# A two-layer transformer on one core: a norm moved across a layer's end, roots and evictions reordered, and one weight load split in ten

## The chip, the core and the metric

The kernel runs on one NeuronCore of a Trainium2 chip. The metric is the device time of one execution in microseconds (us), lower is better. The core has four engines that compute and that run side by side: TensorE (PE in the profile; PEld are its weight loads), VectorE (DVE), ScalarE (ACT) and GpSimd (POOL). A fifth, SyncE (SP), issues loads and stores here. Each engine takes its instructions in the order of its own queue and waits where an operand isn't ready. TensorE writes its products to PSUM, a small memory of banks, from where ScalarE or VectorE copy them out ("evict" them); a bank can be used again only when that is done.

## The reference

`x` is 4 x 512 x 256. Everything is in 32-bit floats. Each of two layers adds an attention and a feed-forward part, both behind a normalisation without weights:

```python
x = x + _L0_attn_ref(_layernorm(x, axis=-1), w_project, w_out)
x = x + _L0_ffn_ref(_layernorm(x, axis=-1), router_w, router_b, expert_w, expert_b)
x = x + _L1_attn_ref(_layernorm(x, axis=-1), w_qkv, w_proj)
x = x + _L1_ffn_ref(_layernorm(x, axis=-1), gate_W_packed, gate_scales, ...)
```

Layer 0's attention is causal, with 16 heads of 16, over 512 positions. Layer 0's feed-forward has 8 experts and a router that gives, for each row and each of the 256 output columns, 8 logits; the two greatest are kept with their softmax weights:

```python
logits = (h @ router_w.T + router_b).reshape(T, O, E)
w, sel = top_k(softmax(logits), 2)
w = w / sum(w)                       # c: these weights, at their experts
final = einsum('te,teo->to', c, einsum('th,eoh->teo', h, expert_w) + expert_b)
```

Layer 1's attention has 16 query heads of 128 in 4 groups, each group with one key and value head. It attends over the first axis of its input, which here has 4 places, so each softmax is over 4 scores. Layer 1's feed-forward multiplies with weights given as packed 4-bit codes and block scales, with a GELU and a gate between.

## The kernel before

**Tiling.** The 2048 rows are 16 groups of 128 (`g`), and 4 blocks of 4 groups (`j` or `b`). `xres` holds the running sum of all of them in the core's memory from beginning to end. A norm is made for one block: `norm_pieces` (line 187) has four statistics pairs on VectorE (L197, L198), a reciprocal root, and four subtract-and-multiply `xn` (L211). The root starts with three small VectorE operations (`rsqrt_guess`) and goes on with ten more (`rsqrt_steps`, L174 to L183) on the engine it is given: GpSimd unless `eng` says VectorE. Then TensorE transposes `xn` in two halves (L227), and ScalarE copies them to `xT` (L294 and L292 in layer 0, L905 in layer 1).

**Order.** TensorE, VectorE and GpSimd run in the order in which the program emits instructions; from layer 1 on ScalarE does too (in layer 0 the framework orders ScalarE). That order comes from a planner. Work that may be put between other work is written as generators, each held in a `Stream`: before a piece it yields `need(engine, cost, gap, cond)`. A call of `fill` (line 140) begins a new slot, gives TensorE and VectorE a budget of microseconds, emits what was deferred, and goes through `streams` in order: a stream may go on while its engine has budget left, at least `gap` slots have passed since its last piece, and `cond` holds. A budget may be overdrawn by one piece, and the debt is carried over. `defer` puts off a ScalarE instruction to the beginning of the next fill. `normed` is a lock: only one norm lies between its statistics and its transposes at a time.

**Layer 0.** 44 batches of attention run through a fixed sequence (scores `s`, their row maxima `mx` at L653, the shift of the queries at L669, scores again, exponentials L692, mixing `av`), with two fills in each. `divided` (line 731) finishes one sequence's heads: transposes, reciprocal and product on VectorE, transposes, and, after the last sequence of a block, two output products (L764) that are added to `xres` (L773). Then `hidden_pieces(j)` normalises that block for the experts. Streams run beside this: `logit_pieces` (products `lg_ps`, evicted to `lg`), `weight_pieces` (line 371, VectorE: the two greatest of 8 logits and their weights, 17 counted pieces a group), `result_pieces` (expert products `eo`, evicted into `part` with the weights as factors, L339), and `addition_pieces` (L366 to L368). Expert and router products go two experts at a time, 512 columns wide, four matmuls each. They continue until far into layer 1 and are the filler between its own steps.

In `weight_pieces` the gap between the two greatest logits (L401) goes through a tanh and a scaling on ScalarE (`lesser`, L405 and L406, put off by one fill); VectorE reads `th` at L421 and `w1` at L434.

After the last batch, a loop of fills runs until the last `divided` is through. Layer 0's memory is then released, and `w_qkv` (two loads of 1536 KB, one for each half of its rows) and `w_proj` (one of 2048 KB) are loaded into its place.

**Layer 1.** `start_pieces(j)` (line 908) normalises block `j`, transposes it and makes the values `v` (L919). It must be through before the block's first of 4 steps `p = 4 j + kv`; block 0's stands at the very beginning, with fills around it, and `hidden_pieces(3)`, inserted just before, shares the norm's lock with it. A step projects four query heads and a key (`project1`, L937, evicted by ScalarE to `qT` and `kT`), scores, softmax, `mix` (line 999: products `a` in four PSUM tiles, one for each quarter of the rows, then four ScalarE copies to `oT`), and `output` (L1025). In the loop over `p` (line 1073) the output of `p` and the projections of `p + 1` alternate, with a fill (`between`) after each. `qk_ps`, `v_ps`, `lg_ps`, `eo` and the transposes share two PSUM buffers (`ps_dn`): each of them waits until the one before the last has been evicted.

When layer 0's experts are through, `weight_in_pieces` begins to unpack the packed weights for layer 1's feed-forward (`dequant_pieces`, line 833): of a piece, two ScalarE operations, `over` (L855) and `sign` (L860), are put off by one fill each.

Of the kernel before, what the change touches and what calls it, by code (L numbers as in the profile page):

```python
# [32 lines left out]
def tile_transformer(  # L33
# [77 lines left out]
    def need(engine, cost, gap=0, cond=None):  # L111
        return engine, cost, gap, cond
# [18 lines left out]
    streams = []  # L131
    deferred = []

    def defer(emit):

        deferred.append((slot, emit))

    left = {"PE": 0.0, "DVE": 0.0}

    def fill(**budget):  # L140

        nonlocal slot
        slot += 1
        while deferred and deferred[0][0] < slot:
            deferred.pop(0)[1]()
        for engine, b in budget.items():
            left[engine] = min(left[engine], 0.0) + b
        again = True
        while again:
            again = False  # L150
            for stream in list(streams):
                while stream.ready(left):
                    engine, cost = stream.go()
                    left[engine] -= cost
                    again = True
                if stream.next is None:
                    streams.remove(stream)
# [26 lines left out]

    normed = []

    def norm_pieces(j, pool, small, out, deinterleave=False, eng=None, cond=None):

        yield need("DVE", 1.0, cond=lambda: not normed and (cond is None or cond()))
        normed.append(j)  # L190
        st = small.tile([P, 4, 6], F32, tag="ln_st", name=f"ln_st{j}")
        mv = small.tile([P, 4, 2], F32, tag="ln_mv", name=f"ln_mv{j}")
        rs = small.tile([P, 4], F32, tag="ln_rs", name=f"ln_rs{j}")
        for t in range(4):
            if t == 2:
                yield need("DVE", 1.0)
            nc.vector.bn_stats(st[:, t, :], xres[:, 4 * j + t, :])  # L197
            nc.vector.bn_aggr(mv[:, t, :], st[:, t, :])  # L198
        eng = eng or nc.gpsimd
        yield need("DVE", 0.6 if eng is nc.gpsimd else 2.6)  # L200
        v = rsqrt_guess(rs, mv[:, :, 1], small, j)
        rsqrt_steps(eng, rs, v, small, j)
        xn = pool.tile([P, 4, HID], F32, tag="xn", name=f"xn{j}")
        for t in range(4):
            if t % 2 == 0:
                yield need("DVE", 0.9, 2 if not t and eng is nc.gpsimd else 0)
            src, dst = xres[:, 4 * j + t, :], xn[:, t, :]
            if deinterleave:
                src = src.rearrange("p (k two) -> p two k", two=2)
                dst = dst.rearrange("p (two k) -> p two k", two=2)  # L210
            nc.vector.tensor_scalar(  # L211
                dst, src, mv[:, t, 0:1], rs[:, t : t + 1], ALU.subtract, ALU.mult
            )
        out.append(xn)
# [66 lines left out]
    def hidden_pieces(b):  # L281

        out = []
        done = (4 * b - 5, 1)
        yield from norm_pieces(b, b1, b2, out, cond=lambda: b < 2 or done in halves)
        xT = b2.tile([P, 2, 512], F32, tag="xT", name=f"xT{b}")
        for hc in range(2):
            yield need("PE", 0.5, 1 - hc)
            ps = transposed(out[0], hc, ps_dn, "dn", f"xT_ps{b}_{hc}")
            ps = ps.rearrange("p t q -> p (t q)")  # L290
            if hc:
                nc.scalar.activation(xT[:, hc, :], ps, AF.Identity, bias=last_16)  # L292
            else:
                nc.scalar.copy(xT[:, hc, :], ps)  # L294
        normed.clear()
        xTs[b] = xT
# [74 lines left out]
    def weight_pieces():  # L371

        tt, stt = nc.vector.tensor_tensor, nc.vector.scalar_tensor_tensor
        for g in range(NT):
            yield need("DVE", 1.25, cond=lambda: g in logits and logits[g][1] < slot)
            d = logits[g][0]
# [27 lines left out]
            def lesser(th=th, gap=gap, w1=w1):  # L404
                nc.scalar.activation(th, gap, AF.Tanh, scale=0.5)  # L405
                nc.scalar.activation(w1, th, AF.Identity, bias=half_t, scale=0.5)  # L406

            defer(lesser)
            for e in (0, 4):
                yield need("DVE", 1.25)  # L410
                tt(  # L411
# [3 lines left out]

            yield need("DVE", 0.7, 1)
            owing = b5.tile([P, HID], F32, tag="owing", name=f"owing_{g}_")
            nc.vector.tensor_scalar(gap, gap, 0.0, -1.0, ALU.is_equal, ALU.mult)  # L420
            stt(owing, th, -1.0, gap, ALU.add, ALU.add)  # L421
# [19 lines left out]
            stt(c1, sums[:, :NE], 0.5, c1, ALU.mult, ALU.add)  # L441
            weights[g] = c1, slot
            del logits[g]

# [6 lines left out]
    with ExitStack() as l0:  # L451
# [343 lines left out]
        for n in range(NBT):  # L795
# [29 lines left out]
            if n in (2, 6):  # L825
                load_x(n // 4 + 2)
        mixed(NBT - 1)
        last = Stream(divided(*batches[NBT - 1][:2]))
        streams.insert(0, last)
        while last.next is not None:  # L830
# [2 lines left out]
    def dequant_pieces(pool, once, n, packed, scales, to, defer=defer):  # L833

        wi = pool.tile([P, 2, HID], I32, tag="dq_w", name=f"dq_w{n}")
        sc = pool.tile([P, 2, HID], F32, tag="dq_s", name=f"dq_s{n}")
        for i in range(2):  # L840
            nc.sync.dma_start(out=wi[:, i], in_=packed[i])
            for b in range(8):
                nc.sync.dma_start(out=sc[16 * b : 16 * b + 16, i], in_=scales[i](b))
        mi = once.tile([P, 2, 2, HID], I32, tag="dq_m", name=f"dq_m{n}")
        si = once.tile([P, 2, 2, HID], I32, tag="dq_i", name=f"dq_i{n}")
        a = once.tile([P, 2, 2, HID], F32, tag="dq_a", name=f"dq_a{n}")
        over = once.tile([P, 2, 2, HID], F32, tag="dq_b", name=f"dq_b{n}")
# [12 lines left out]
        defer(lambda: nc.scalar.activation(sign, si, AF.Identity, bias=half_t, scale=-0.125))  # L860
        yield need("DVE", 1.25)
        stt(a, mi, 4.0, mi, ALU.max, ALU.add)
        yield need("DVE", 1.25, 1)
        stt(a, a, -4.0, over, ALU.add, ALU.add)
        yield need("DVE", 1.25)
        tt(a, a, sign, ALU.mult)
        yield need("DVE", 1.3)
        tt(to, a, sc.unsqueeze(2).to_broadcast([P, 2, 2, HID]), ALU.mult)
# [16 lines left out]
    with ExitStack() as l1:  # L885
        in_order.enter_context(tc.manual_schedule(engines={mybir.EngineType.Activation}))
        wb = l1.enter_context(tc.tile_pool(name="w_l1", bufs=1))
        wqkv = wb.tile([P, 2, NKV, HPK + 2, P], F32, name="wqkv")
        for hc in range(2):
            nc.sync.dma_start(out=wqkv[:, hc], in_=w_qkv[hc * P : (hc + 1) * P])  # L890
        wpj = wb.tile([P, NKV * HPK, HID], F32, name="wpj")
        nc.sync.dma_start(out=wpj, in_=w_proj.rearrange("(e p) h -> p e h", p=P))
        c1 = l1.enter_context(tc.tile_pool(name="l1_1", bufs=1))
# [6 lines left out]
        def into_T(out, to, name):  # L900

            for hc in range(2):
                yield need("PE", 0.5, 1 - hc)
                ps = transposed(out[0], hc, ps_dn, "dn", f"{name}_ps{hc}")
                nc.scalar.copy(to[:, hc, :], ps.rearrange("p t q -> p (t q)"))  # L905
            normed.clear()

        def start_pieces(j):

            out = []  # L910
            yield from norm_pieces(j, c1, c1, out, cond=lambda: (4 * j + 3, 1) in added)
            xT = c2.tile([P, 2, 512], F32, tag="xT", name=f"xT1_{j}")
            yield from into_T(out, xT, f"xT1_{j}")
            v = c2.tile([P, 4, NKV, P], F32, tag="v", name=f"v{j}")
# [84 lines left out]
        def mix(p):  # L999
# [10 lines left out]
                    )  # L1010
            oT = c2.tile([P, HPK, 512], F32, tag="oT", name=f"oT{p}")
            oq = oT.rearrange("p h (t c q) -> p c t h q", c=NC, q=32)
            for c in range(NC):
                nc.scalar.copy(oq[:, c], avs[c])
            state["o"] = oT

        def output(p, t):

# [54 lines left out]
        for p in range(-1, NP):  # L1073
# [22 lines left out]
            for h in range(HPK + 1):  # L1096
                if h == 2 and p >= 0:
                    mix(p)
                    if not new:
                        first_products()  # L1100
                if new:
                    project1(p + 1, h)
                    between()
            for t in range(4):
                if p >= 0:
# [20 lines left out]
    with ExitStack() as f1:  # L1126
# [9 lines left out]
        def inner(j):  # L1136
            xT = normed_T(j, d2, d2, ps_dn, "dn", deinterleave=True) if j else x_first
            it = d2.tile([P, NJ, 2, 512], F32, tag="it", name=f"it{j}")
            for jj in range(NJ):
# [21 lines left out]
                if j < 2 and jj % 4 == 3:  # L1161
                    at = 4 * j + 2 * (jj // 4)
                    for _ in dequant_pieces(
                        d2, d1, f"d{at}", [down_w[at + i] for i in range(2)],
                        [
                            lambda b, i=i: down_s[at + i, b : b + 1, :].to_broadcast([16, HID])
                            for i in range(2)
                        ],
                        wd[:, at : at + 2], lambda emit: emit(),
                    ):  # L1170
                        pass
            return it
# [85 lines left out]
```

## Time and profile before

| | us |
|---|---|
| median of 3 runs | 1230.52 (1230.14 to 1233.79) |
| the profiled execution | 1231.27 |
| its span | 1229.6 |

Busy time by stretch, of the profiled execution:

| stretch, us | what runs | PE | DVE | ACT | PE clock |
|---|---|---|---|---|---|
| 0 to 165 | attention of layer 0, first blocks | 141.7 | 90.0 | 55.2 | 0.95 |
| 165 to 403 | attention with router and experts | 228.2 | 204.5 | 130.4 | 0.99 |
| 403 to 431 | end of layer 0 | 23.2 | 21.5 | 13.6 | 1.00 |
| 431 to 491 | start of layer 1 | 50.9 | 35.7 | 21.9 | 0.86 |
| 491 to 745 | attention of layer 1 with experts | 251.7 | 169.8 | 113.1 | 0.99 |
| 745 to 900 | attention of layer 1 with unpacking | 150.9 | 102.5 | 62.4 | 1.00 |
| 900 to 1229.6 | feed-forward of layer 1 | 325.6 | 188.6 | 87.1 | 1.00 |

How to read the profile: one execution was recorded instruction by instruction. Times count from the start of the span. L12 is line 12 of the kernel. "out<-in" names what an instruction writes and reads. The "releaser" of an idle time is the instruction whose end let the waiting one go. The clock is the share of TensorE's full clock that it was granted. DVE is VectorE, ACT is ScalarE, POOL is GpSimd, SP is SyncE.

### The profile page before, as it was taken

What the parts mean: (1) busy time and instruction counts of PE and PEld (TensorE: products, weight loads), DVE (VectorE), ACT (ScalarE), POOL (GpSimd) and SP (SyncE); (2) the same over time, 40 slices, a digit from 0 to 9 for tenths busy, and PEclk for the clock granted to TensorE, in tenths of its full rate; (3) what the DMA queues carried; (4) which work ended last, traced back from release to release, by engine and by line L of the source; (5) the groups of instructions that cost most, each with busy time, mean ns of one, the idle gap of its engine ahead of it and who ended that gap; (6) DMA issues with size and microseconds to landing.
All of it is one profiled execution on the core that took longest, in us unless ns stands there. A gap on an engine that the chain in (4) does not pass through costs nothing.

```text
span 1229.6 us, 18921 instructions
## 1 busy us (share of the span) xinstructions
PE 1172.0 (95%) x7278; PEld 682.0 (55%) x7278; DVE 812.5 (66%) x1862; ACT 483.7 (39%) x1101; POOL 131.3 (11%) x249
## 2 busy tenths in 40 slices
PE   6888999999999897999999999999999999999998
PEld 3666555555545443555555555555645456475487
DVE  3655589887889838395967396588589962734710
ACT  1243455555555533344444344345234431312300
POOL 7343422111121001000000000100000000000000
PEclk9899999999999988999999999999999999999999
DMA  6031102000000310000000001011010000000000
GB/s 201 5 100 35 19 1 36 1 1 2 1 2 2 117 55 1 1 1 1 1 1 1 1 1 35 10 43 53 1 50 19 1 1 17 1 1 18 0 1 35
DMA packets 19386, 26.78 MB, mean 22 GB/s; under 512 B 4992, under 2 KB 13440, under 8 KB 19040
## 3 DMA queue, kind: packets, MB, share of 16 engines
q1 hardware_dynamic: 18624, 24.40, 7.0%
q10 hardware_dynamic: 672, 1.18, 0.4%
q8 instruction: 57, 0.93, 0.3%
q14 instruction: 33, 0.27, 0.1%
HBM read 19.27 MB, written 2.10 MB: 17 GB/s over the span
## 4 chain that ended last, share of the span: by engine, by line
PE 77%; DVE 16%; ACT 3%; DMA 2%; issue 1%; POOL 1%; SPq 0%; ACTq 0%; DVEq 0%; POOLq 0%
PE qk_ps L937 10%; PE y L1178 9%; PE g L874 9%; PE u L874 9%; PE o L1025 8%; PE lg_ps L251 7%; PE eo L251 6%; PE s L633 4%; DVE mx L653 3%; PE s L683 2%; PE v_ps L919 2%; PE qk_ps L548 2%; PE av L719 2%; PE s L950 1%; DVE lg L411 1%
## 5 line engine op out<-in xcount | busy, mean ns | idle before, releaser
L937 PE MATMUL qk_ps<-xT,wqkv 128*128 128x512 f32 x320 | 151.3, 604 | 5.0 <-ACT qT L941 5.0
L251 PE MATMUL lg_ps<-rw,xT 128*128 128x512 f32 x256 | 125.7, 614 | 4.4 <-ACT part L339 1.4
L251 PE MATMUL eo<-ew,xT 128*128 128x512 f32 x256 | 122.8, 605 | 1.9 <-ACT part L339 1.9
L1025 PE MATMUL o<-wpj,oT 128*128 128x256 f32 x512 | 119.4, 382 | 0.0
L653 DVE TENSOR_REDUCE mx<-s 128x1 f32<-128x384 f32 (+3 forms) x176 | 100.4, 632 | 18.3 <-PE s L648 18.3
L1178 PE MATMUL y<-wd,it 128*128 128x256 f32 x512 | 112.1, 379 | 0.0
L1025 PEld LDWEIGHTS o<-wpj,oT 128*128 128x128 f32 x512 | 96.0, 190 | 28.2 <-issue 16.4
L1178 PEld LDWEIGHTS y<-wd,it 128*128 128x128 f32 x512 | 97.0, 190 | 15.6 <-issue 2.9
L937 PEld LDWEIGHTS qk_ps<-xT,wqkv 128*128 128x128 f32 x320 | 59.7, 192 | 75.3 <-issue 61.8
L692 ACT ACTIVATE pt<-s 128x512 f32<-128x512 f32 (+1 forms) x176 | 83.7, 561 | 35.7 <-PE s L683 35.6
L874 PE MATMUL g<-xT,wgu 128*128 128x512 f32 x192 | 90.5, 593 | 0.0
L874 PE MATMUL u<-xT,wgu 128*128 128x512 f32 x192 | 90.2, 592 | 0.0
L702 POOL TENSOR_SCALAR_AFFINE_SELECT pt<-pt 128x256 f32<-128x256 f32 (+2 forms) x88 | 56.7, 651 | 267.1 <-ACT pt L692 266.7
L339 ACT ACTIVATE part<-eo,c 128x256 f32<-128x256 f32 x128 | 53.7, 472 | 78.9 <-PE eo L251 78.9
L1156 ACT ACTIVATE th<-sq 128x512 f32<-128x512 f32 x64 | 40.3, 630 | 88.6 <-DVE sq L1155 88.6
L251 PEld LDWEIGHTS eo<-ew,xT 128*128 128x128 f32 x256 | 47.6, 193 | 48.5 <-issue 40.9
L251 PEld LDWEIGHTS lg_ps<-rw,xT 128*128 128x128 f32 x256 | 46.7, 194 | 49.8 <-issue 38.4
L633 PE MATMUL s<-qk 32*128 32x128 f32 (+3 forms) x512 | 67.0, 496 | 2.6 <-ACT pt L692 1.9
L239 DVE TENSOR_TENSOR xres<-xres,y 128x256 f32<-128x256 f32 x16 | 6.7, 420 | 91.3 <-PE y L1178 91.3
L313 ACT COPY lg<-lg_ps 128x512 f32<-128x512 f32 x64 | 37.7, 589 | 71.2 <-PE lg_ps L251 71.2
L366 DVE TENSOR_TENSOR part<-part 128x512 f32<-128x512 f32 x32 | 21.9, 684 | 65.5 <-ACT part L339 65.4
L941 ACT COPY qT<-qk_ps 128x512 f32<-128x512 f32 x64 | 37.8, 593 | 61.4 <-PE qk_ps L937 61.4
(254 smaller groups left out, 1820.2 us busy)
## 6 DMA issues: line engine op xcount, KB each, us to landing
qk<-stage SPq DMA_DIRECT2D x56, 64.0 KB, 2.4
wqkv<-in_w_qkv SPq DMA_DIRECT2D x2, 1536.0 KB, 8.3
rw<-in_router_w SPq DMA_DIRECT2D x8, 256.0 KB, 4.6
ew<-in_expert_w SPq DMA_DIRECT2D x8, 256.0 KB, 4.8
wpj<-in_w_proj SPq DMA_DIRECT2D x1, 2048.0 KB, 15.4
out<-xres SPq DMA_DIRECT2D x4, 512.0 KB, 2.6
xres<-in_x SPq DMA_DIRECT2D x3, 512.0 KB, 7.1
dq_wgu<-in_gate_w SPq DMA_DIRECT2D x8, 128.0 KB, 2.4
```

The source lines that it names most:

```text
L251: nc.tensor.matmul(ps, lhsT=xT[:, hc, (g % 4) * P : (g % 4 + 1) * P], rhs=w[:, hc, 2 * pair : 2 * pair + 2, :].rearrange("p e o -> p (e o) ...
L339: nc.scalar.mul(part[:, e % 4], ps[:, i], c[:, e : e + 1])
L633: nc.tensor.matmul(tiles[h][:, b * nk : (b + 1) * nk].rearrange("p (c k) -> p c k", k=P), lhsT=queries(j, g)[r, s], rhs=qk[r, g, : j + 1, ...
L653: nc.vector.tensor_reduce(maxes[n % 2][:, :nb, h, 0], ps[:, : nb * nk].rearrange("p (b k) -> p b k", b=nb), AX.X, ALU.max,)
L692: nc.scalar.activation(pt[:, i, : nb * nk], tiles[2 * pair + i][:, : nb * nk], AF.Exp, scale=0.25)
L702: nc.gpsimd.affine_select(out=last, in_=last, compare_op=ALU.is_ge, fill=0.0, base=0, pattern=pattern, channel_multiplier=-1,)
L874: nc.tensor.matmul(ps, lhsT=wgu[:, w, half, jj, par * P : (par + 1) * P], rhs=xT[:, half, :], start=half == 0, stop=half == 1,)
L937: nc.tensor.matmul(ps, lhsT=wqkv[:, hc, kv, h, :], rhs=xT[:, hc, :], start=hc == 0, stop=hc == 1,)
L941: nc.scalar.copy(kT if h == HPK else qT[:, h, :], ps)
L1025: nc.tensor.matmul(ys[t // 2][:, t % 2], lhsT=state["o"][:, h, t * P : (t + 1) * P], rhs=wpj[:, HPK * kv + h, :], start=kv == 0 and h == 0 ...
L1156: nc.scalar.activation(th, sq, AF.Tanh, scale=0.7978845608028654)
L1178: nc.tensor.matmul(ps, lhsT=it[:, c // 2, c % 2, t * P : (t + 1) * P], rhs=wd[:, c // 2, c % 2, :], start=c == 0, stop=c == 2 * NJ - 1,)
```

## The change

- `defer` takes a number of slots; what is deferred is emitted at the beginning of the fill in which it falls due. `lesser` and `sign` are put off by two fills instead of one, and VectorE's next pieces wait for that.
- Block 0's norm for layer 1 is a stream of its own, started after layer 0's last batch, in front of all but the last `divided`, with its root on VectorE and its result in `normed_first`. `start_pieces(0)` begins with the transposes.
- The last `hidden_pieces` has its root on VectorE, and its transposes at least two slots after `xn`. The transposes of `start_pieces` and of layer 1's feed-forward, too, come two slots after `xn` instead of one, and `xn` of blocks 1 to 3 three slots after the root's start instead of two; the two halves of a transposed block follow each other as before.
- `w_qkv` is loaded in ten pieces: the values' columns of all four groups (two halves of the rows), then for each group its query and key columns (two halves).
- The four `oT` copies aren't emitted together after `mix`: two are, one follows the third query projection of the next step, and one the fourth. In the last step all four stay together.

```diff
@@ -131,9 +131,9 @@
-    def defer(emit):
-
-        deferred.append((slot, emit))
+    def defer(emit, slots=1):
+
+        deferred.append((slot + slots, emit))
@@ -141,8 +141,9 @@
         slot += 1
-        while deferred and deferred[0][0] < slot:
-            deferred.pop(0)[1]()
+        for due in [d for d in deferred if d[0] <= slot]:
+            deferred.remove(due)
+            due[1]()
@@ -184,7 +185,7 @@
-    def norm_pieces(j, pool, small, out, deinterleave=False, eng=None, cond=None):
+    def norm_pieces(j, pool, small, out, deinterleave=False, eng=None, cond=None, wait=2):
@@ -203,7 +204,7 @@
-                yield need("DVE", 0.9, 2 if not t and eng is nc.gpsimd else 0)
+                yield need("DVE", 0.9, wait if not t and eng is nc.gpsimd else 0)
@@ -282,10 +283,14 @@
-        yield from norm_pieces(b, b1, b2, out, cond=lambda: b < 2 or done in halves)
+        last = b == NBLK - 1
+        yield from norm_pieces(
+            b, b1, b2, out, eng=nc.vector if last else None,
+            cond=lambda: b < 2 or done in halves,
+        )
...
-            yield need("PE", 0.5, 1 - hc)
+            yield need("PE", 0.5, 0 if hc else 1 + last)
@@ -404,8 +410,9 @@
                 nc.scalar.activation(w1, th, AF.Identity, bias=half_t, scale=0.5)
-
-            defer(lesser)
+                lessers.append(th)
+
+            defer(lesser, 2)
@@ -415,7 +422,8 @@
-            yield need("DVE", 0.7, 1)
+            yield need("DVE", 0.7, 1, cond=lambda: lessers)
+            lessers.clear()
@@ -825,6 +835,7 @@
         mixed(NBT - 1)
+        streams.insert(0, Stream(norm_pieces(0, b1, b2, normed_first, eng=nc.vector)))
         last = Stream(divided(*batches[NBT - 1][:2]))
@@ -857,12 +868,12 @@
-        defer(lambda: nc.scalar.activation(sign, si, AF.Identity, bias=half_t, scale=-0.125))
+        defer(lambda: nc.scalar.activation(sign, si, AF.Identity, bias=half_t, scale=-0.125), 2)
...
-        yield need("DVE", 1.25)
+        yield need("DVE", 1.25, 1)
         tt(a, a, sign, ALU.mult)
@@ -886,8 +897,16 @@
-        for hc in range(2):
-            nc.sync.dma_start(out=wqkv[:, hc], in_=w_qkv[hc * P : (hc + 1) * P])
+
+        for kv, i in [(slice(None), slice(HPK + 1, HPK + 2))] + [
+            (slice(kv, kv + 1), slice(0, HPK + 1)) for kv in range(NKV)
+        ]:
+            for hc in range(2):
+                tc.keep_in_program_order(
+                    nc.sync.dma_start(
+                        out=wqkv[:, hc, kv, i], in_=w_qkv[hc * P : (hc + 1) * P, kv, i]
+                    )
+                )
@@ -900,15 +919,18 @@
-                yield need("PE", 0.5, 1 - hc)
+                yield need("PE", 0.5, 0 if hc else 2)
...
-            out = []
-            yield from norm_pieces(j, c1, c1, out, cond=lambda: (4 * j + 3, 1) in added)
+            out = [] if j else normed_first
+            if j:
+                yield from norm_pieces(
+                    j, c1, c1, out, cond=lambda: (4 * j + 3, 1) in added, wait=3
+                )
@@ -1010,9 +1032,12 @@
-            for c in range(NC):
-                nc.scalar.copy(oq[:, c], avs[c])
             state["o"] = oT
+            state["a"] = [lambda c=c: nc.scalar.copy(oq[:, c], avs[c]) for c in range(NC)]
+
+        def mixed_out(n):
+            for _ in range(n):
+                state["a"].pop(0)()
@@ -1096,10 +1121,13 @@
                     mix(p)
+                    mixed_out(2 if new else NC)
                     if not new:
                         first_products()
                 if new:
                     project1(p + 1, h)
+                    if h in (2, 3) and p >= 0:
+                        mixed_out(1)
                     between()
```

More of the change, by code (lines that the diff above doesn't have):

```diff
@@ L373, in weight_pieces @@
         tt, stt = nc.vector.tensor_tensor, nc.vector.scalar_tensor_tensor
+        lessers = []
         for g in range(NT):
@@ L443, in weight_pieces @@
             del logits[g]
+    normed_first = []
     with ExitStack() as l0:
@@ L1168, in inner @@
                         ],
-                        wd[:, at : at + 2], lambda emit: emit(),
+                        wd[:, at : at + 2], lambda emit, slots=1: emit(),
                     ):
```

## The prediction

> **What bounds the kernel now.** First the page: busy time, then the slices.
>
> ```profile
> PE 1172.0 (95%) x7278; PEld 682.0 (55%) x7278; DVE 812.5 (66%) x1862; ACT 483.7 (39%) x1101; POOL 131.3 (11%) x249
> PE   6888999999999897999999999999999999999998
> PEclk9899999999999988999999999999999999999999
> ```
>
> TensorE (PE) is busy 1172.0 of 1229.6 us, so only its idle time, and time at a lower clock, can be removed. Both digits dip at the start and again in slices 14 to 16 (430 to 492 us): layer 0 hands over to layer 1 there. The changed lines lie in the second dip. The view of waits, TensorE alone, names those of its waits that the change can reach:
>
> ```profile
> PE xT_ps L227 <- DVE xn L211: 7.8, 3, 3.2
> PE qk_ps L937 <- ACT qT L941: 5.0, 6, 2.1
> PE v_ps L919 <- ACT xT L905: 1.6, 1, 1.6
> PE v_ps L919 <- ACT v L923: 1.3, 1, 1.3
> ```
>
> Columns: total us, times, longest. The timeline shows where they are (start, duration, in brackets the idle time before and its releaser):
>
> ```profile
> 406.19 0.69 DVE L366 TENSOR_TENSOR part<-part 128x512 f32<-128x512 f32 x1 [3.31 <-ACT part L339]
> ...
> 431.39 1.76 PE L227 MATMUL xT_ps<-ident,xn 128*128 128x128 f32 x8 [1.84 <-DVE xn L211]
> ...
> 434.72 9.54 PE L919 MATMUL v_ps<-wqkv,xT 128*128 128x512 f32 x16 [1.56 <-ACT xT L905]
> ...
> 465.65 1.89 PE L227 MATMUL xT_ps<-ident,xn 128*128 128x128 f32 x8 [3.21 <-DVE xn L211]
> ...
> 483.75 2.20 PE L227 MATMUL xT_ps<-ident,xn 128*128 128x128 f32 x8 [2.73 <-DVE xn L211]
> ...
> 736.22 0.42 ACT L405 ACTIVATE th<-gap 128x256 f32<-128x256 f32 x1 [2.77 <-DVE gap L401]
> ...
> 737.08 2.03 ACT L1014 COPY oT<-a 128x512 f32<-128x512 f32 x4
> ...
> 739.65 3.50 PE L937 MATMUL qk_ps<-xT,wqkv 128*128 128x512 f32 x4 [2.09 <-ACT qT L941]
> ```
>
> Three norms (layer 1 block 0 at 431, layer 0's last block at 465, layer 1 block 1 at 483) make the in-order TensorE stand. At 739 ScalarE (ACT) stood 2.77 us for `gap`, then copied all four `oT` before the `qT` copy whose PSUM buffer TensorE wanted.
>
> A stall also costs after it ends. Four 512-column matmuls take 1.9 us normally and 3.50 at 739. Busy time by window shows why (PE, PEld, DVE, ACT, POOL, then granted clock):
>
> ```profile
> 429.36:432.77 3.41, 1.57 (x9) 0.93 (x8) 2.19 (x8) 1.41 (x6) 1.03 (x5) 1.00 1.07 358
> 432.77:436.18 3.41, 1.84 (x5) 0.86 (x4) 3.34 (x13) 2.03 (x7) 0.00 (x0) 0.50 0.74 235
> ...
> 463.49:466.90 3.41, 1.25 (x6) 0.79 (x7) 3.26 (x10) 0.26 (x2) 0.00 (x0) 1.00 0.00 0
> ...
> 480.56:483.97 3.41, 0.68 (x3) 0.14 (x1) 1.03 (x4) 0.59 (x1) 1.93 (x9) 1.00 0.00 0
> 483.97:487.38 3.41, 2.37 (x9) 1.68 (x9) 3.38 (x15) 1.93 (x6) 0.00 (x0) 0.50 0.00 0
> ...
> 736.56:739.97 3.41, 1.32 (x4) 0.47 (x3) 3.34 (x6) 3.38 (x9) 0.00 (x0) 1.00 0.00 0
> ...
> 787.76:791.17 3.41, 1.81 (x4) 0.87 (x5) 1.43 (x3) 2.04 (x5) 1.54 (x5) 1.00 0.00 0
> ```
>
> After a window with TensorE busy 1.57 us or less of 3.41, the next runs at half clock; after 1.81 it doesn't. At half clock, windows busy 1.84 and 2.37 kept it there, a full one ended it.
>
> **A rule against the row.** The Trainium skill ("TensorE: Matmul & The Clock Gate", "HAM oscillation — how this bites in real kernels") warns of idle gaps over about 3.4 us. The longest here is 3.21, so by that rule no clock is lost and the change is worth the idle time alone. The rows show half clock after gaps of 1.84, 2.09, 2.73 and 3.21. I take the rows. What the reachable stalls cost, idle plus half of the busy time at half clock:
>
> - A, 431: 1.84 + 1.56 + (1.84 + 3.42)/2 = 6.0
> - B, 465: 3.21 + 3.42/2 = 4.9
> - C, 483: 2.73 + 1.04 (at 487, for xT) + (2.37 + 3.42)/2 = 6.7
> - D, 739: 2.09 + 3.41/2 = 3.8
> - E, three waits at half past 745 to 860 (787, 806, 855): 1.73 + 1.31 + 0.45 = 3.5
>
> Together 24.9, of which 9.0 is clock; the rule would leave 15.9.
>
> **The change, part by part.**
>
> *Block 0's norm inside layer 0.* It moves 4 statistics pairs (0.41 + 0.18 each, started 0.53 apart: 2.3 us), the root and 4 `xn` (1.4) ahead of the last `divided`. On VectorE the root's ten small operations have rows of about 0.16; with 0.04 between, 2.0, plus 0.6 for the three before. Of these 4.9 us of statistics and root, the 3.31 us hole before 406.19 takes most: VectorE ended at 402.9, so the root ends near 408.0, and the reciprocal of `divided`, at 408.40 before, isn't late.
>
> The planner's budget is another matter. VectorE gets 2.6 a fill; statistics 2.0 and root 2.6 put it at -2.0. Number the fills after the last batch F1 to F7. The addition moves from F1 to F3, group 6's weights are complete in F6 instead of F3, and until then neither an expert product nor the next logit is allowed: before, F1, F2, F3, F5, F6 and F7 carried a product each, now F1, F2, F6 and F7. TensorE then runs `divided` tight, its second output product ending near 415.4 instead of 419.8, but the first expert product waits for the PSUM buffer that VectorE's residual add frees, behind two 1.2 us maxima and minima of group 7: about 2.3 us near 417. With 0.7 for the `aT` copy that is 3.0 against 1.9 (0.46 + 0.47 + 0.93) before: cost 1.1. If it empties one window below 1.6 us it adds 1.7; half a chance, 0.9.
>
> In layer 1 the transposes come in the second fill, with `xn` long done; the first carries an expert product. `v_ps`, the fill after, still waits about 1.1 for the `xT` copy. So A gains 6.0 - 1.1 - 1.1 - 0.9 = 2.9 (bounds 2.1 and 3.8; 0 if the starvation is worse).
>
> *Roots and gaps.* The last `hidden_pieces` has its root on VectorE: 2.0 us there, in a stretch where it is busy 35.7 of 60 us, instead of 2.8 on GpSimd (456.47 to 459.23). Its `xn` can now be queued one fill after the root, and its transposes two fills after `xn`. By the planner it starts in the fill that makes group 7's last product, `xn` follows in the next, and the first transpose lies five TensorE pieces later, some 4 us after `xn`. Block 1's norm keeps GpSimd but `xn` comes three fills after the root and the transposes two later, roughly 17 us of other work for a 2.8 to 4.6 us root. What is queued behind the waiting transposes is all of TensorE, so B and C were wholly on the path: B + C = 11.6, less 0.6 for leftovers, 11.0. Enough products exist to cover (65 are left at layer 1's start in the old order, 69 in the new).
>
> *Ten loads.* Old: two loads issued at 419.84 land at 426.47 and 430.20, read first at 434.72; hidden. The new first reader comes near 425, issued near 415.5: the two old loads would have landed 6.6 and 10.4 later, near 422 and 426, a wait of 1. The new order sends the two V parts, 256 KB each, first. SP pays eight more issues at 0.42, 3.4 us, and `w_proj`, behind them, lands at about 415.5 + 4 + 15.4 = 435, long before its first use near 470. Cost 0; a bound of 1 if even the V parts are late.
>
> *Two, one, one.* The four `oT` copies cost the same (0.60 each). Between them now stand a `qT` copy and what the fill emitted. The last is emitted a whole projection before `output`. *Tanh one fill later*: ScalarE stood 23.8 us for `gap` in twelve waits; only the one at 736 reached TensorE. *The sign of the dequantisation one fill later* splits 1.15 + 1.14 us of ScalarE (785 to 787), which caused 787 and 806. D + E = 7.3. Each can recur where a 1.15 copy meets `oT` and `qT` in one fill (1.15 + 0.60 + 0.59 = 2.3, over the 1.72 of a projection), so I take 3.3 of D and 2.0 of E; bounds 0 and 7.3.
>
> *Price of the late tanh.* VectorE reads `th` at L421. In layer 0, from tanh's start to L420, the first seven groups have 6.0, 5.7, 6.1, 6.3, 8.2, 6.3 and 6.7 us. Less 0.97 for tanh and `w1` the margin is 5.5 in the mean, 4.8 at least. A fill there is 4.0 us (57 fills from 165.1 to 391.6). It fits, unless four exponentials (2.06) go in front: then up to 1.3 a group on VectorE, busy 204.5 of 238 us. Bounds 0 and 9; I take 1.0. In layer 1 margins are shorter (two groups have none), perhaps 10 us of VectorE waits, beside 84 us of its idle time in 254: nothing, but 1.0 for collisions the new order brings.
>
> Sum: 2.9 + 11.0 + 3.3 + 2.0 - 1.0 - 1.0 = **17.2 us**. The profiled execution (1231.27, of it 1229.6 span) becomes 1214.1; the median of the runs is 0.75 lower, so **1213.3**.
>
> **Rivals.** *R1, starvation.* At the end of layer 0 the lost products idle TensorE as long as the norm did: A gives nothing, 1216.2. For: four products where six stood. Against: work moved, not lost. *R2, ScalarE's edits only shift their collisions*: D and E give nothing, 1218.6; for it speaks that D and E were coincidences of one group or one dequantisation. Both together: 1221.5. *R3, slower.* Tanh misses VectorE's reads in layer 0, where `mx` and `qk` of the attention stand behind L420. It decides from 17.2/7 = 2.5 us a group. If tanh slips two fills and the exponentials, 7.9 + 2.1 - 5.5 = 4.5 us, seven groups cost 31 and the time is 1245. Against: one fill is what the edit asks, and VectorE never waited there before. *R4*: the norm of block 0 finds VectorE so late that `divided` slips with it, and A, B and C move rather than go: 3.3 are left, 1227, which counts as no change. Against: the hole before 406.19.
>
> **Numbers.** Forecast 0.56, R1 0.12, R2 0.16, R1 with R2 0.04, R3 0.07, R4 0.05. A measurement tells 0.3%, 3.7 us, from no change. All but R3 and R4 are faster: 0.88; R4 is the same, 0.05; R3 slower, 0.07. The range runs from everything gained without cost (3.8 + 11.6 + 7.3 = 22.7, 1207.8) to R1 with R2, rounded: 1207 to 1222.
>
> **What would show it.** Right: L227's wait for `xn` falls from 7.8 to under 1.5; no half clock between 440 and 500; layer 1's first `v_ps` starts near 425 instead of 434.7; `mxT` and `av` of layer 0 keep their times to 1 us at 403. R1: TensorE idle over 3 us between 411 and 420, with half clock after it. R2: waits of L937 for `qT` still near 5 us. R3: waits of VectorE at L420 for `th` over 10 us before 403. I am wrong if the handover to layer 1 brings a stall I didn't list, or if layer 0 before 403 changes by more than 3 us.

## The result, and the profile after

| | changed | before, same chip |
|---|---|---|
| median of 6 runs, us | 1214.15 (1210.02 to 1216.14) | 1231.86 (1230.14 to 1233.79) |
| ratio, 95% interval | 0.9851 (0.9836 to 0.9865) | |
| the profiled execution | 1210.02 (span 1208.2) | 1231.27 (span 1229.6) |

The change is worth 17.7 us; 17.2 were forecast, 1213.3 against 1214.15. The two profiled executions lie further apart, 21.4 us of span, because the profiled execution of the changed kernel is the fastest of its six, with a mean granted clock of 0.991. The others, 1212.45 to 1216.14 us, had 0.985 to 0.989. So the steps are measured against 21.4, and the gap to 17.7 is taken up at the end.

The page of the changed kernel: span, busy time, slices.

```profile
span 1208.2 us, 18944 instructions
PE 1161.2 (96%) x7278; PEld 676.8 (56%) x7278; DVE 815.0 (67%) x1882; ACT 485.0 (40%) x1101; POOL 127.7 (11%) x229
PE   6888999999999899999999999999999999999998
PEclk9999999999999999999999999999999999999999
```

TensorE has the same 7278 instructions in 10.8 us less busy time (mostly because fewer of them ran at half clock), and the dip of its clock in slices 15 and 16 is gone. GpSimd lost twenty operations to VectorE, the two roots. The waits of TensorE that answer to those of before (total us, times, longest):

```profile
PE qk_ps L959 <- ACT xT L924: 2.2, 2, 2.0
PE qk_ps L959 <- ACT qT L963: 1.6, 2, 1.4
PE v_ps L941 <- ACT v L945: 1.4, 1, 1.4
PE o L774 <- ACT aT L765: 0.7, 1, 0.7
PE eo L252 <- ACT lg L318: 0.7, 1, 0.7
```

The wait of the transposes for `xn`, 7.8 us before, has no row any more. The wait for `qT` fell from 5.0 to 1.6. One row is new in kind: `qk_ps` waits 2.0 us for an `xT` copy. The timeline places them (start, duration, in brackets the idle time before and its releaser):

```profile
407.33 0.25 DVE L753 RECIPROCAL rden<-av_T 128x16 f32<-128x16 f32 x1
411.25 3.72 PE L774 MATMUL o<-wo,aT 128*128 128x256 f32 x16 [0.73 <-ACT aT L765]
...
417.37 3.70 PE L252 MATMUL eo<-ew,xT 128*128 128x512 f32 x8 [0.68 <-ACT lg L318]
...
422.00 0.66 PE L228 MATMUL xT_ps<-ident,xn 128*128 128x128 f32 x4 [0.49 <-ACT part L344]
422.49 5.40 PE L941 MATMUL v_ps<-wqkv,xT 128*128 128x512 f32 x12
429.25 1.98 PE L941 MATMUL v_ps<-wqkv,xT 128*128 128x512 f32 x4 [1.36 <-ACT v L945]
...
484.09 0.42 ACT L435 ACTIVATE spare<-owing 128x256 bf16<-128x256 f32 x1 [1.59 <-DVE owing L445]
...
484.78 0.42 ACT L435 ACTIVATE spare<-owing 128x256 bf16<-128x256 f32 x1 [0.17 <-DVE owing L445]
...
485.87 1.05 ACT L924 COPY xT<-xT_ps 128x512 f32<-128x512 f32 x2
...
486.49 1.98 PE L959 MATMUL qk_ps<-xT,wqkv 128*128 128x512 f32 x4 [2.01 <-ACT xT L924]
...
795.18 3.70 PE L959 MATMUL qk_ps<-xT,wqkv 128*128 128x512 f32 x8 [1.40 <-ACT qT L963]
```

VectorE made the norm in its hole, and `divided`'s reciprocal stood at 407.33. The first `v_ps` came at 422.49 instead of 434.72. The wait at 429 is for a PSUM buffer whose copy to `v` stood in ScalarE's queue behind three sums of the weight pieces (L435), the first of which waited 1.71 us for VectorE. The wait that ends at 486 is the one stall that the new order brought: the copies to `xT` (485.87) stand behind three such sums, and those wait for `owing`, which VectorE makes.

The stretch at the start of layer 1, before and then after (PE, PEld, DVE, ACT, POOL busy, then the granted clock):

```profile
431.00:491.00 60.00, 50.88 (x173) 23.47 (x174) 35.66 (x105) 21.91 (x50) 5.79 (x20) 0.86 0.08 24
```

```profile
431.00:491.00 60.00, 57.64 (x248) 29.76 (x247) 40.55 (x119) 26.67 (x64) 4.15 (x10) 1.00 0.02 6
```

In the same 60 us TensorE has 75 more instructions, at full clock.

**Where the 21.4 us came from.** TensorE comes to layer 0's last `av` at 402.67 instead of 403.03, so 21.0 fell later. From there to the end its idle time went from 24.4 to 13.4 us, which is 11.0. The windows at half clock, 20.5 us long with 17.9 of TensorE's work in them, went altogether; at full clock that work takes half as long, which is 8.9. Together 19.9; TensorE's busy time fell by another 1.1 us, for which no window at half clock accounts.

### The profile page after: what moved, and what is told of

The parts are those of the page before. It is cut to its first block, busy times and chain, and to the rows that moved or that the text cites. A ratio compares the mean times of both kernels' runs of the same rounds, so it can differ in the third digit from the quotient of the medians.

```text
span 1208.2 us, 18944 instructions
## 1 busy us (share of the span) xinstructions
PE 1161.2 (96%) x7278; PEld 676.8 (56%) x7278; DVE 815.0 (67%) x1882; ACT 485.0 (40%) x1101; POOL 127.7 (11%) x229
## 4 chain that ended last, share of the span: by engine, by line
PE 76%; DVE 18%; ACT 3%; issue 1%; DMA 1%; POOL 0%; SPq 0%; ACTq 0%; DVEq 0%; POOLq 0%
PE qk_ps L959 9%; PE y L1206 9%; PE g L885 9%; PE u L885 9%; PE o L1050 8%; PE lg_ps L252 7%; PE eo L252 6%; DVE mx L663 4%; PE s L643 3%; PE s L693 2%; PE qk_ps L558 2%; PE av L729 2%; DVE lg L418 2%; PE v_ps L941 1%; PE a L1030 1%
## 5 line engine op out<-in xcount | busy, mean ns | idle before, releaser
L318 ACT COPY lg<-lg_ps 128x512 f32<-128x512 f32 x64 | 37.6, 588 | 83.6 <-PE lg_ps L252 83.6
L643 PE MATMUL s<-qk 32*128 32x128 f32 (+3 forms) x512 | 64.4, 485 | 2.6 <-ACT pt L702 1.9
L885 PEld LDWEIGHTS u<-xT,wgu 128*128 128x128 f32 x192 | 36.5, 190 | 45.9 <-issue 44.7
L1185 DVE SCALAR_TENSOR_TENSOR th<-th,g 128x512 f32<-128x512 f32 x63 | 43.1, 685 | 28.3 <-ACT th L1184 28.2
```

The lines of the kernel that those rows point to most:

```text
L643: nc.tensor.matmul(tiles[h][:, b * nk : (b + 1) * nk].rearrange("p (c k) -> p c k", k=P), lhsT=queries(j, g)[r, s], rhs=qk[r, g, : j + 1, ...
L885: nc.tensor.matmul(ps, lhsT=wgu[:, w, half, jj, par * P : (par + 1) * P], rhs=xT[:, half, :], start=half == 0, stop=half == 1,)
L1185: nc.vector.scalar_tensor_tensor(th, th, 1.0, gp, ALU.add, ALU.mult)
```

## The experiments

The main theory is the prediction's: the gain is the sum of the stalls A to E, each with its half-clock time, removed by the part of the change named beside it. Its rivals: the parts are not independent (one part removes another's stall by shifting the plan); the clock is not lost to these stalls (the rule of 3.4 us that the prediction sets against the row); the ten loads do nothing. Times are medians of four to seven executions; the ratio is to the kernel before on the same chip, with its 95% interval.

### The three ScalarE edits: taken out, and alone

The edits: `defer(lesser, 2)` back to `defer(lesser)`, `sign` put off by one fill (with VectorE's pieces behind both where they were), the four `oT` copies together. The first kernel is the changed one without them:

```diff
-            defer(lesser, 2)
+            defer(lesser)
...
-        defer(lambda: nc.scalar.activation(sign, si, AF.Identity, bias=half_t, scale=-0.125), 2)
+        defer(lambda: nc.scalar.activation(sign, si, AF.Identity, bias=half_t, scale=-0.125))
...
-                    mixed_out(2 if new else NC)
+                    mixed_out(NC)
...
-                    if h in (2, 3) and p >= 0:
-                        mixed_out(1)
```

> The changed kernel with its three ScalarE edits undone (tanh and sign one fill after, the four oT copies together). Theory: the norm, the roots, the gaps and the ten loads give some 13 us of the 17.7; the time is near 1219, and TensorE again waits about 2 us for a qT copy behind four oT copies near 720 us, with half clock after it, and in the unpacking. Rival (the ScalarE edits only shift their collisions): as the changed kernel, near 1214.

Measured: 1215.94 us, ratio 0.9877 (0.9858 to 0.9896). The intervals of this and of the changed kernel overlap. TensorE's idle time from 745 to 900 us came back (4.9 against 2.0), but the stall D did not: without the ScalarE edits, the earlier norms alone shifted the plan so that tanh and the four copies no longer met. They lie 7.6 us apart:

```profile
718.46 2.05 ACT L1036 COPY oT<-a 128x512 f32<-128x512 f32 x4 [0.43 <-PE a L1030]
...
726.03 0.42 ACT L411 ACTIVATE th<-gap 128x256 f32<-128x256 f32 x1
```

A smaller wait came in another place, 1.27 us at 652 for a `v` copy, without half clock after it.

The second kernel is the one before with those three edits and nothing else.

> The kernel before with the three ScalarE edits alone. Theory: about 5 us faster than before, near 1227, the stalls at 431, 465 and 483 unchanged. Rival (collisions only shift): no change, 1232. Rival (the late tanh holds VectorE up): slower than 1232.

Measured: 1226.90 us, 0.9952 (0.9936 to 0.9968), 4.9 us faster. Here D is gone, TensorE's idle time from 745 to 900 is 2.0 instead of 4.1, and the waits for `xn` remain, 8.1 us in three. So these edits do remove D and half of E when they stand alone; beside the others only E is still theirs. D is counted twice if the parts are added.

### Block 0's norm alone

The changed kernel without the ScalarE edits, and with the last `hidden_pieces` and the gaps between root and `xn` as before:

```diff
-        last = b == NBLK - 1
-        yield from norm_pieces(
-            b, b1, b2, out, eng=nc.vector if last else None,
-            cond=lambda: b < 2 or done in halves,
-        )
+        yield from norm_pieces(b, b1, b2, out, cond=lambda: b < 2 or done in halves)
...
-            yield need("PE", 0.5, 0 if hc else 1 + last)
+            yield need("PE", 0.5, 1 - hc)
...
-                    j, c1, c1, out, cond=lambda: (4 * j + 3, 1) in added, wait=3
+                    j, c1, c1, out, cond=lambda: (4 * j + 3, 1) in added, wait=2
```

It keeps the two slots between `xn` and the transposes of layer 1's blocks.

> The kernel before with block 0's norm inside layer 0 and the ten loads, and nothing else but the gap of two slots in layer 1's transposes. Theory: the stall at 431 with its half clock goes and some 1 us of new idle time before it comes, 4 to 5 us, near 1227; the stall of the last hidden block stays. Rival (the end of layer 0 is starved of products instead): within 1 us of 1232.

Measured: 1220.62 us, 0.9903 (0.9886 to 0.9920): 11.2 us faster, more than twice what was expected. The timeline and the waits of TensorE in this kernel say why:

```profile
462.97 1.31 PE L228 MATMUL xT_ps<-ident,xn 128*128 128x128 f32 x4 [1.68 <-DVE xn L212]
```

```profile
PE qk_ps L955 <- ACT v L941: 3.5, 1, 3.5
PE xT_ps L228 <- DVE xn L212: 1.7, 1, 1.7
```

B is halved (1.68 instead of 3.21, with one window at half clock still behind it) with the same root on GpSimd, probably because the norm's lock comes free earlier; that was not tried by itself. C is gone but for 0.68 us: its transposes come two slots after `xn`, and the third slot before `xn` isn't needed for that. D is gone here too. A stall of 3.5 us at 792, with two half-clock windows behind it (6.8 us), is new: two `v` copies stand in ScalarE's queue behind `over` and `sign` of the unpacking, and `over` waits for VectorE. The changed kernel doesn't have it.

### Roots and gaps alone

The kernel before with the root of the last `hidden_pieces` on VectorE, `wait=3`, and the two-slot gaps; block 0's norm in layer 1 and two loads, as before.

```diff
-            yield need("PE", 0.5, 1 - hc)
+            yield need("PE", 0.5, 0 if hc else 1 + last)
...
-                yield need("PE", 0.5, 1 - hc)
+                yield need("PE", 0.5, 0 if hc else 2)
...
-            yield from norm_pieces(j, c1, c1, out, cond=lambda: (4 * j + 3, 1) in added)
+            yield from norm_pieces(
+                j, c1, c1, out, cond=lambda: (4 * j + 3, 1) in added, wait=3 if j else 2
+            )
```

> The kernel before with the last hidden block's root on VectorE, three slots for the roots of blocks 1 to 3 and two slots before the transposes, and nothing else. Theory: the stalls at 465 and 483 with their half clock go, about 10 us, near 1222; the one at 431 stays. Rival (they move, since block 0's norm still stands ahead of both on the lock): under 4 us, 1228 or more.

Measured: 1219.57 us, 0.9897 (0.9880 to 0.9914), 12.2 us faster. B and C are gone but for 1.44 us, and A stays with 2.10 + 1.84 us idle and 6.8 us at half clock. The gain is near the 11.0 for B and C, but it isn't theirs alone: D (3.8) went with them, and two waits of 1.21 us, at 725 and 732, are new. The block norm alone and this kernel together give 23.4, while the kernel that has both without the ScalarE edits gives 15.8: most of C, some 6 us, lies in both, and so does D; the new stall of the block norm alone hides a part of that. Which of root and gaps removes B was not separated.

### Two loads instead of ten

```diff
-        for kv, i in [(slice(None), slice(HPK + 1, HPK + 2))] + [
-            (slice(kv, kv + 1), slice(0, HPK + 1)) for kv in range(NKV)
-        ]:
-            for hc in range(2):
...
+        for hc in range(2):
+            tc.keep_in_program_order(
+                nc.sync.dma_start(out=wqkv[:, hc], in_=w_qkv[hc * P : (hc + 1) * P])
+            )
```

> The changed kernel with w_qkv in the two loads of before. Theory: the second half lands about 10.4 us after its issue at 415, near 425.5, while the first v_ps starts at 422.5 in the changed kernel: TensorE waits some 3 us there for the load, with half clock after it where the window falls so; 3 to 5 us slower than the changed kernel, 1217 to 1219. Rival (the split is worth nothing, since the load was hidden before): as the changed kernel, 1214.

Measured: 1214.04 us, 0.9841 (0.9816 to 0.9866): no difference from the changed kernel. The loads do come too late, as expected, issued at 418.5 and landing at 425.1 and 428.9, and the timeline shows the wait:

```profile
429.04 3.24 PE L936 MATMUL v_ps<-wqkv,xT 128*128 128x512 f32 x7 [1.96 <-DMA wqkv<-in_w_qkv]
```

But it takes the place of the 1.36 us for the `v` copy, which is done meanwhile, so the net loss is 0.6 us, which these rounds can't show. The ten loads are as free as forecast, and bring next to nothing while the `v` copy is late.

### TensorE kept busy through the stalls

The kernel before, with matmuls whose result nothing reads: two, three and three of 512 columns in front of the three late transposes, and one behind each of layer 1's two. The norms stay where they are and are waited for as before; only the share of the time in which TensorE works rises.

```diff
+    def keep_busy(n):
+        ps = spare_psum[0].tile([P, 4, HPK, 32], F32, tag="a", name=f"busy_{slot}_{n}")
+        for _ in range(n):
+            nc.tensor.matmul(
+                ps.rearrange("p t h q -> p (t h q)"), lhsT=ident,
+                rhs=xres[:, 0:2, :].rearrange("p g h -> p (g h)"), start=True, stop=True,
+            )
```

> The kernel before, with matmuls on xres whose products nobody reads, put in front of the three late transposes (2, 3 and 3 of 0.86 us) and one behind each of layer 1's two: nothing that is waited for comes earlier. Theory (the clock follows TensorE's busy share of 3.41 us windows): half clock between 430 and 491 us goes, about 7 us faster than before, near 1225. Rival (the rule of gaps over 3.4 us; the half clock has another cause): no gain, 1232 or more.

Measured: 1227.06 us, 0.9955 (0.9938 to 0.9971), 5.1 us faster with more work. The same stretch of this kernel:

```profile
431.00:491.00 60.00, 55.94 (x200) 25.09 (x199) 36.30 (x108) 24.64 (x59) 6.96 (x26) 1.00 0.11 36
```

The clock is 1.00 where it was 0.86. By the windows of the kernel before, the half-clock part of A, B and C was (1.84 + 3.42 + 3.42 + 2.37 + 3.42)/2 = 7.2 us; a new wait of 1.56 us at 475 takes some of it back. This settles the rule against the row: with all idle gaps under 3.4 us, clock was lost, and filling the windows with matmuls brought it back.

### What stands in the changed kernel

Four more runs look for what the stalls left are worth. A stall of layer 0, in both kernels, lies at 343 to 348: the second transposed half of block 2 waits 1.65 us for a PSUM buffer that the first half holds, and 0.78 follow. The edit puts one slot between these halves:

```diff
-            yield need("PE", 0.5, 0 if hc else 1 + last)
+            yield need("PE", 0.5, int(b == 2) if hc else 1 + last)
```

> The changed kernel, with one slot between the two transposed halves of layer 0's block 2. Theory: the second half waited 1.65 us at 343 for the first one's copy, as the other PSUM buffer was held by an open av_T; a slot later VectorE has freed it. The stall of 1.65 + 0.78 us and the half clock after it go: 2 to 4 us faster than the changed kernel, 1210 to 1212. Rival: the wait moves to another product, no change.

Measured: 1209.27 us, 0.9807 (0.9785 to 0.9829), under the changed kernel by 4.9 us as first measured, and by 2.7 us as measured again on this chip (below). All its executions (1206.53 to 1209.96) lie under all of the changed kernel's (1210.02 to 1216.72). Its waits of TensorE have this row:

```profile
PE lg_ps L252 <- ACT xT L299: 1.6, 1, 1.6
```

The 1.65 us only moved to the router's product, but the 0.78 and the half clock after it are gone. The profiles tell the gain apart from the spread of the executions: from batch 33's `av` to batch 37's, with the stall between them, both recorded executions of the changed kernel take 35.1 us, and both recorded with this slot (here and with the later sums in layer 1, below) 32.3, 2.8 less.

The next edit puts the four sums off by two fills everywhere, so that no `xT` or `v` copy stands behind a sum that isn't ready:

```diff
-                defer(sum_up)
-                yield need("DVE", 0.95, cond=lambda: len(deferred) < 4)
+                defer(sum_up, 2)
+                yield need("DVE", 0.95, cond=lambda: len(deferred) < 7)
...
-            yield need("DVE", 0.3, 1)
+            yield need("DVE", 0.3, 2)
```

> The changed kernel with the sums on ScalarE (L435) put off by two fills instead of one. Theory: they wait less for VectorE in ScalarE's queue, and the copies behind them come in time: the stalls at 428 (1.36, v_ps) and 484 (2.01, qk_ps) go, 2 to 5 us faster than the changed kernel. Rival: weights of each group are complete one slot later and products run short: slower.

Measured: 1213.75 us, 0.9850 (0.9828 to 0.9873), no gain. The stalls at 428 and 484 are gone, which shows their cause; but layer 0, whose plan it changes as well, has 34 us at half clock instead of 20 and new stalls near 222, 250, 330 and 370.

The next two and the changed kernel again ran on one chip. First the changed kernel with all four `oT` copies together (`mixed_out(NC)`, as in the first diff, the other ScalarE edits kept):

> The changed kernel with the four oT copies together again, the tanh and the sign still put off by two fills. Theory: the waits of projections for qT copies in the unpacking come back, some 2 to 3 us in all: 1216 to 1217. Rival (with the tanh put off nothing else stands in front of the copies): as the changed kernel, 1214.

Measured: 1214.50 us, 0.9856 (0.9835 to 0.9878). Idle from 745 to 900 us doubles, 4.0 instead of 2.0, but the times can't be told apart from the changed kernel's. As `sign` and tanh are late here, the 2.0 us of E that the change removed belong to the copies. Then the sums put off by two fills in layer 1 only, with the slot in block 2:

```diff
-                defer(sum_up)
-                yield need("DVE", 0.95, cond=lambda: len(deferred) < 4)
+                defer(sum_up, 2 if in_layer_1 else 1)
+                yield need("DVE", 0.95, cond=lambda: len(deferred) < (7 if in_layer_1 else 4))
...
-            yield need("DVE", 0.3, 1)
+            yield need("DVE", 0.3, 2 if in_layer_1 else 1)
...
+        in_layer_1.append(1)
```

> The changed kernel with one slot between the transposed halves of block 2, and the sums on ScalarE put off by two fills in layer 1 alone. Theory: the stalls of 1.36 at 424 and 2.02 at 481 go as well, with nothing moved in layer 0: 2 to 3 us under the kernel with block 2's halves apart alone, 1206 to 1207. Rival: late weights put other waits in their place: 1209 or more.

Measured: **1206.19 us**, 0.9789 (0.9769 to 0.9810). TensorE's idle time from 403 to 500 us is 2.7, while it is 6.8 in the changed kernel on this chip (next), and the stalls at 429 and 484 are gone. This version beats both kernels. Last, the changed kernel on this chip:

> The changed kernel as it is, beside the two others on the same chip: 1212 to 1216 by both theories; the yardstick for differences of a few us.

Measured: 1212.00 us (1211.58 to 1216.72), 0.9844 (0.9818 to 0.9869). Its profile shows the stall at 484 with the clock lost:

```profile
485.25:488.66 3.41, 1.40 (x11) 1.08 (x10) 3.04 (x14) 2.32 (x8) 0.00 (x0) 1.00 0.00 0
488.66:492.07 3.41, 3.41 (x5) 1.37 (x5) 0.00 (x0) 0.26 (x2) 0.00 (x0) 0.50 0.00 0
```

## The prediction against the runs

The mechanism held: stalls of TensorE at the handover went, with the half clock behind them. A, B and C went by the norms' part of the change, and E by the split copies; D went with the norms too, not by the late tanh or the copies. The terms, all measured in the two profiles:

| term | forecast | measured | why |
|---|---|---|---|
| A, block 0's norm | 2.9 | 4.6 | waits 411 to 423: 1.90 after, 1.86 before; `v_ps` then 1.36 |
| B + C, roots and gaps | 11.0 | 9.6 | 2.01 left at 484, not 0.6 |
| D, tanh and the four copies | 3.3 | 3.8 | gone altogether, but with the norms |
| E, `sign` and copies | 2.0 | 2.1 | idle 745 to 900: 4.1 to 2.0 |
| price of the late tanh | -2.0 | 0 | no wait that TensorE saw |
| sum | 17.2 | 20.1 | of 21.4 in the profiles |

**A.** The use of VectorE's hole was right: the reciprocal stood at 407.33, no later than the 408.0 reckoned for the root's end. The starvation priced at 1.1 us, and the chance of a half-clock window at 0.9, did not come: the first expert product waited 0.68 us near 417, not 2.3, and for an `lg` copy, not behind VectorE's maxima. The wait of `v_ps` was 1.36 for 1.1, but it is the `v` copy behind three sums that made it.

**B and C.** Gone as said. What I missed is that earlier transposes bring the copies to `xT` to a place where ScalarE's queue holds three sums that wait for VectorE. The rule that I used for TensorE, to ask what is queued ahead and what that waits for, I didn't apply to ScalarE. The runs with later sums show the cause. So a sign that I had named for being wrong, an unlisted stall at the handover, did come: 2.01 us where 0.6 was set aside, and some 1.7 more in the second execution, which has a window at half clock behind it. The range had room for it. The other signs were met: the first `v_ps` at 422.49 (near 425 was said), and `av` 0.35 us earlier at 403.

**D and E.** The sizes held, the credit for D did not. The run without the ScalarE edits shows that D goes by the shift of the plan alone. R2 had named it a coincidence, and expected collisions to come back elsewhere. None of D's size did in that run; smaller ones did (1.27 us there, two of 1.21 with roots and gaps alone), and with the block norm alone a larger one (3.5).

**The late tanh.** Priced at 1.0 in layer 0 and 1.0 in layer 1; both nothing. In layer 0 the framework orders ScalarE and put the tanh where it had been: its waits for `gap` are the same to 0.01 us (1.77 in both kernels, then 2.27 and 2.28). Emission order there isn't execution order, and this edit changed nothing. In layer 1 VectorE waited for `th` twice, 2.14 us at 501 and 2.55 at 561, and TensorE didn't notice.

**The rivals.** R1: TensorE's idle between 411 and 420 was 0.73 + 0.68, without half clock. R2: the waits for `qT` are 1.6, not 5. R3: no wait for `th` before 403. R4: the reciprocal wasn't late.

**The clock.** The rule that I read from the rows, half clock after 1.57 us of TensorE in a window but not after 1.81, priced the stalls of layer 1. It isn't exact, and it fails in layer 0; the last section has the numbers.

**Why the total fits better than its terms.** The profiles lie 21.4 us apart, the medians 17.7: executions of one kernel differ. Four recorded executions share the changed kernel's order in layer 0:

| | us at half clock before 403 | last `av` of layer 0 starts |
|---|---|---|
| changed kernel | 20.5 | 403.66 |
| with copies together | 23.9 | 405.73 |
| changed kernel again | 27.3 | 405.57 |
| with two loads | 37.6 | 407.15 |

So layer 0 alone can make 3.5 us of the spread of the six runs (6.1), though not in step with its half clock. The changed kernel's second recorded execution has a span 3.6 us longer than the first: 1.9 lie before that `av`, and 1.7 behind it, as much as the half clock after the stall at 484 costs. So part of the agreement within 1 us is luck: the terms were some 3 us too small together, and the typical execution is 4 us longer than the profiled one (1214.15 against 1210.02). The granted clock of the other five, 0.985 to 0.989 against 0.991, fits this; where each of them lost its time isn't recorded.

## What to carry to other kernels

Price a stall of the bounding engine with the clock that it costs afterwards, window by window: here that was 8.9 of 21.0 us. In an order made by a planner, parts of a change are not additive; take one out and put one in alone before crediting it, and expect a stall that is a meeting of two things to go when either moves, and others to come. When a step is moved earlier, ask of every in-order queue that its copies enter, not only of the bounding engine's, what stands ahead and what that waits for.

## What the runs showed of the hardware

In the thirteen profiles every stretch at half clock is 3.41 or 6.83 us long: the clock is granted in windows of 3.41 us. They don't begin with the program's steps, so the same stall may or may not cost clock. The stall at 343 to 348, by window, in the kernel before and then in the changed one (PE, PEld, DVE, ACT, POOL, then granted clock):

```profile
344.02:347.43 3.41, 1.76 (x27) 1.40 (x20) 3.34 (x5) 2.54 (x5) 1.81 (x2) 1.00 0.00 0
347.43:350.84 3.41, 2.63 (x11) 1.04 (x13) 0.74 (x1) 1.01 (x2) 0.20 (x1) 1.00 0.00 0
```

```profile
342.99:346.40 3.41, 1.08 (x8) 0.60 (x6) 3.12 (x4) 2.66 (x6) 2.02 (x2) 1.00 0.00 0
346.40:349.81 3.41, 3.31 (x4) 1.17 (x4) 0.00 (x0) 0.05 (x1) 0.00 (x0) 0.50 0.00 0
```

The work is the same. Before, the boundary splits the stall, neither window falls under 1.76 us of TensorE, and the clock stays; after, one window gets nearly all of it, 1.08 us are left busy, and the next runs at half clock, 3.31/2 = 1.7 us lost. From batch 33's `av` to batch 37's the two take 33.5 and 35.1 us. The slot in block 2 therefore gains more than the 0.78 us of idle time that it takes away: in the profiles, 17.1 us at half clock before 403 instead of 20.5.

TensorE's busy time doesn't settle it alone. In the kernel before, a window as busy as the one at 344 was followed by half clock:

```profile
279.17:282.58 3.41, 1.77 (x14) 0.68 (x13) 3.38 (x12) 2.06 (x8) 0.63 (x2) 1.00 0.03 7
282.58:286.00 3.42, 3.17 (x4) 1.17 (x4) 3.39 (x11) 0.19 (x1) 0.00 (x0) 0.50 0.00 0
```

In layer 1, over all thirteen profiles, every full-clock window with less than 1.46 us of TensorE was followed by half clock and none with more than 1.74; between the two both occur (1.54 at 483 in the changed kernel kept the clock, 1.57 at 429 in the kernel before lost it). In layer 0 much busier windows lost it: 2.16 us at 169 in the changed kernel, 3.23 at 241 in the one with two loads. In both, attention's score products, with 32 rows, are most of the work; whether that is the reason was not tried. Pricing by windows is shown here for layer 1, with its wide products, and not beyond.
